# Attention and feed-forward block on one core: the value matmuls of one unit issued in two parts

## The chip, the cores and the metric

The kernel runs on one core of a Trainium2 chip. The metric is the time of one execution on the device in microseconds (us). Profiled times come from one execution under the hardware profiler. TensorE (PE) multiplies matrices; its weight loads (PEld) are listed apart. VectorE (DVE), ScalarE (ACT) and GpSimd (POOL) work elementwise, and SyncE (SP) issues DMAs.

## The reference

Input `x` is 8 x 1024 x 512 in float32. One block is computed:

```
x = x + layernorm(attention(layernorm(x)))
x = x + layernorm(ffn(layernorm(x)))

attention(h):  q, v, k = split(h @ Wqvk)           # 16 heads of 32
               scores  = q . k, causal mask, / sqrt(512)
               weights = softmax(scores over the keys)
               return (weights @ v) @ Wo
ffn(x):        hidden = x @ W1 + b1                # 512 -> 2048
               imag   = w_imag * sin(theta + 0.1 * hidden)
               q      = hidden + 0.1 * (cos(theta) * w_real + sin(theta) * w_imag) * imag
               return relu(q) @ W2 + b2
```

## The kernel before

The batch has eight blocks `b` of 1024 rows. For each, `attention` runs over four groups `g` of four heads, and `feed_forward` follows. Projections of the next group, the rest of the previous block's normalisation and parts of this block's output projection are put between the attention's steps by generators (`work`, `more`), which are advanced at fixed points of the loop. The matmuls, and most of the other instructions near the change, are marked `in_order`: they run on their engine in the order in which the code issues them.

A head group goes in two phases. First `find_maxima` computes the scores with queries on the partitions, to find the row maxima. They are split into bf16 parts (`parts_q`), transposed on TensorE and copied to an SBUF tile `mT`, one for each half of the 1024 queries. For the second half the transposes come in the third unit of the loop below, and the copy is made by VectorE (L734).

Then the loop in `attention` takes the keys in units, with the keys on the partitions. The first half of the queries (`c = 0`) sees key tiles 0 to 3 in three units; the second half (`c = 1`) sees all eight in seven. A counter `at` numbers the ten units from 0 to 9:

```
KEY_UNITS = (
    ((0,), (1, 3), (2,)),
    ((0,), (1,), (2,), (3,), (4,), (5, 7), (6,)),
)
```

Key tile `kb` of 128 keys counts only for queries from `kb` on. So in the first half key tile 1 is 384 queries wide, tile 2 is 256 wide and tile 3 is 128 wide. Unit 1 (`at == 1`) holds tiles 1 and 3 side by side in the 512 columns of a bank.

For each unit the loop does the following, in this order:

- `weigh`: TensorE writes minus the maxima (L603, bf16) and adds the scores (L614, f32). Both use the array as four row tiles (32*128 in the profile), one for each head. They fill two PSUM tiles of two banks each, two heads in each. ScalarE then takes the exponential of each tile (L629) into an SBUF tile `w`. GpSimd sets the squares above the diagonal to zero (L633).
- at some units, the transposes or projections.
- `flush`: runs the step that the previous unit left in `late`. It is `weighted_values`: TensorE multiplies the values with the previous unit's weights (L652), with the array as four column tiles (128*32), and adds them up in one PSUM bank `acc`.
- for the second half, `add_weights`: VectorE adds the unit's weights to the running total (L681).

So TensorE's order is: scores of unit n + 1, values of unit n, scores of unit n + 2, values of unit n + 1. An f32 matmul is two passes and shows as two records. Behind the last unit of the first half ScalarE copies `acc` to `wvT` (L767). The second half's result is divided by its sums in `sums`, which runs in the next group.

`psum` chooses banks by the order in which earlier tiles were drained. Of the eight banks, four hold the scores of a unit, and the next unit's second score tile gets the banks that the first exponential of the unit before sets free.

Of the kernel before, what the change touches and what calls it, by code (L numbers as in the profile page):

```python
# [31 lines left out]
def kernel(  # L32
# [48 lines left out]
    def psum(shape, dtype=F32):  # L81
        size = math.prod(shape[1:]) * (2 if dtype == BF16 else 4)
        n = -(-size // (4 * HALF))
        free = [k for k in range(0, 8, n) if None not in done_at[k : k + n]]

        def rank(k):
            halved = n == 1 and done_at[k ^ 1] is None and done_at[k] + 2 <= clock[0]
            return not halved, max(done_at[k : k + n])

        k = min(free, key=rank)  # L90
        t = banks[:, k : k + n, :].rearrange("p b n -> p (b n)")[:, : size // 4]
        if dtype != F32:
            t = t.bitcast(dtype)
        if len(shape) == 3:
            t = t.rearrange("p (a b) -> p a b", a=shape[1])
        done_at[k : k + n] = [None] * n
        banks_of[id(t)] = list(range(k, k + n)), t
        return t

    def drained(t, n=None):  # L100

        mine = banks_of[id(t)][0]
        for k in [mine[0]] if n is None and len(mine) == 1 else mine if n is None else [mine[n]]:
            clock[0] += 1
            done_at[k] = clock[0]

    def in_order(instruction):
        tc.keep_in_program_order(instruction)
# [180 lines left out]
    def advance(work, steps=1):  # L289
        for _ in range(steps):  # L290
            if next(work, None) is None:
                return

    def finish(work):
        for _ in work:
            pass
# [283 lines left out]
    def transpose_maxima(parts, evacuate):  # L580
        pt = psum([P, TPB, P], BF16)
        for n in range(TPB):
            transpose_on_pe(pt[:, n, :], parts[:, n, :], ident_h)
        mT = small.tile([P, HALF], BF16, tag="mT", name="mT", bufs=2)
        evacuate(mT, pt.rearrange("p n t -> p (n t)"))
        drained(pt)
        return mT
# [58 lines left out]
    def weighted_values(acc, b, g, first, last, weights, placed):  # L646

        for k, (kb, cols, n) in enumerate(placed):
            for j in range(HPG):
                r = slice(j * HD, (j + 1) * HD)  # L650
                in_order(
                    nc.tensor.matmul(  # L652
                        acc[r, HALF - n :],
                        v[b, g][:, kb, r],
                        weights[j // 2][:, j % 2, cols],
                        start=first and k == 0,
                        stop=last and k == len(placed) - 1,
                    )
                )

    def weight_sums(acc, weights, placed):

        for k, (_, cols, n) in enumerate(placed):
            for j in range(HPG):
                r = slice(j * HD, (j + 1) * HD)
                in_order(
                    nc.tensor.matmul(  # L667
                        acc[r, HALF - n :],
                        ones,
                        weights[j // 2][:, j % 2, cols],  # L670
                        start=(k == 0),
                        stop=(k == len(placed) - 1),
                    )
                )

    def add_weights(total, weights, placed):

        for t, w in zip(total, weights):
            for _, cols, n in placed:
                q = slice(HALF - n, HALF)  # L680
                in_order(nc.vector.tensor_add(t[:, :, q], t[:, :, q], w[:, :, cols]))  # L681

    def divide(acc, total, dst):

        inverse = tmp.tile([P, HALF], F32, tag="tmp", name="inverse")
        in_order(nc.scalar.activation(inverse, total, AF.Ln))
        drained(total)
        in_order(nc.scalar.activation(inverse, inverse, AF.Exp, scale=-1.0))
        in_order(nc.vector.tensor_tensor(dst, acc, inverse, ALU.mult))
        drained(acc)  # L690

    def attention(b, wvT, after):

        late = [None]
        summing = [None]

        def sums():
            if summing[0] is not None:  # L700
                summing[0]()
                summing[0] = None

        def flush():
            if late[0] is not None:
                late[0]()
                late[0] = None

        def projections(g):
            if g + 1 < NG:  # L710
                return project_qkv(b, g + 1)
            if g + 1 == NG and b + 1 < B:
                return project_qkv(b + 1, 0)
            return iter(())

        work = projections(0)
        for g in range(NG):
            more, first = after(g)
            mT, later = find_maxima(b, g, work, sums, iter(()) if g and first is not None else more)
            mTs = [mT]  # L720
            at = 0
            for c in range(2):
                accs = []
                total = None
                units = KEY_UNITS[c]
                for u, keys in enumerate(units):
                    later(at)
                    weights, placed = weigh(b, g, c, keys, mTs[c])
                    if at < 2:
                        advance(work)  # L730
                    if at == 2:
                        mTs.append(
                            transpose_maxima(
                                parts_q[1], lambda *a: in_order(nc.vector.tensor_copy(*a))  # L734
                            )
                        )
                    if c and u == len(units) - 2:
                        finish(work)
                        work = projections(g + 1)
                    if c and u >= len(units) - 2:  # L740
                        advance(work)
                    if first is None and (at < 2 or c and u >= len(units) - 2):
                        advance(more)
                    flush()


                    if c and u == 0:
                        total = weights, placed
                    elif c:
                        add_weights(total[0], weights, placed)  # L750

                    def step(accs=accs, u=u, last=u == len(units) - 1, weights=weights, c=c, g=g,
                             placed=placed, total=total, dst=wvT[c][:, g, :]):
                        if u == 0:
                            accs.append(psum([P, HALF]))
                        acc = accs[0]
                        weighted_values(acc, b, g, u == 0, last, weights, placed)
                        if last and c:

                            def whole():  # L760
                                whole_sum = psum([P, HALF])
                                weight_sums(whole_sum, *total)
                                divide(acc, whole_sum, dst)

                            summing[0] = whole
                        elif last:
                            nc.scalar.copy(dst, acc)  # L767
                            drained(acc)

                    late[0] = step  # L770
                    if first is not None and at >= first:
                        advance(more)
                    at += 1
            flush()
            if g == NG - 1:
                advance(more)
                sums()
            else:
                finish(more)
        return more  # L780
# [177 lines left out]
    for b in range(B):  # L958
# [4 lines left out]
        def after(g, b=b, wvT=wvT, x2T=x2T, rest=rest):  # L963


            if g == 0:
                return rest, len(KEY_UNITS[0])
            if (b, g) == (0, 1) and B > 1:
                ahead = measure_ahead(1, (2, 2, 1, 0, 0, 0, 2, 1))
                advance(ahead)  # L970
                return ahead, 2
            if g == NG - 2 and b + 1 < B:
                return norm1(b + 1), None
            if g == NG - 1:
                return finish_block(b, 0, wvT[0], x2T), len(KEY_UNITS[0]) + 1
            return iter(()), 0
# [47 lines left out]
```

## Time and profile before

| | |
|---|---|
| time, median of 3 runs | 3862.25 us (3861.39 to 3862.28) |
| the profiled execution's own time | 3861.85 us |
| its span, first to last instruction | 3860.1 us |
| mean granted TensorE clock | 0.995 |
| PE busy | 3799.7 us (98%) |
| DVE busy | 2743.9 us (71%) |
| ACT busy | 1541.5 us (40%) |
| POOL busy | 576.3 us (15%) |
| DMA | 86.43 MB, mean 22 GB/s |

The profile is that of one execution. In a line of a group, the columns are the line of the code with engine, operation, what is written from what, shape and count; then the busy time in us and the mean of one in ns; then the engine's idle time before these instructions and what released it. In a timeline they are start (us from the start of the span), duration, engine, line and operation; in square brackets the idle time before it and the releaser. Successive pieces of a timeline can overlap a little, since matmuls and elementwise instructions are pipelined and the ends of matmuls are modelled.

### The profile page before, as it was taken

Reading aid. Unit: us, or ns where it says so; the run is one execution under the profiler, and the core shown is the slowest. Engines: PE = TensorE matmul, PEld = TensorE weight load, DVE = VectorE, ACT = ScalarE, POOL = GpSimd, SP = SyncE. Lnnn points to the kernel's source line nnn. Section 1 sums busy time; section 2 is a strip of 40 time slices with the busy share of each in tenths; the row PEclk is TensorE's granted clock in tenths of the full one; section 3 lists DMA queues with packets and bytes.
Section 4 is the critical chain, followed back from the end, with each engine's and each line's share of the span. In section 5 each row is a group of like instructions: output and inputs, shape, how many; then the busy total and the mean of one; then the engine's idle time right before and its main releaser. Section 6 shows DMA issues by size and latency. Waiting matters only on the chain. (4 is left out here: it accounts for less than half of the span.)

```text
span 3860.1 us, 51461 instructions
## 1 busy us (share of the span) xinstructions
PE 3799.7 (98%) x19457; PEld 1767.7 (46%) x19457; DVE 2743.9 (71%) x6105; ACT 1541.5 (40%) x2960; POOL 576.3 (15%) x1060
## 2 busy tenths in 40 slices
PE   8999999999999999999999999999999999999998
PEld 4544445444444444444444444444445444454443
DVE  4867767677676777767777767777677776777666
ACT  4552146521465214642156421564215641156311
POOL 1211021110211102210022100222002120022100
PEclk9999999999999999999999999999999999999999
DMA  4100000000000001000010000000001000000000
GB/s 156 34 12 23 22 31 15 12 22 22 31 15 12 22 22 33 12 12 22 22 34 12 12 22 22 34 12 13 21 22 34 12 12 0 22 23 12 1 0 22
DMA packets 45081, 86.43 MB, mean 22 GB/s; under 512 B 4192, under 2 KB 7328, under 8 KB 44320
## 3 DMA queue, kind: packets, MB, share of 16 engines
q1 hardware_dynamic: 38480, 70.57, 5.6%
q10 hardware_dynamic: 6352, 12.58, 0.9%
q8 instruction: 152, 2.49, 0.3%
q14 instruction: 97, 0.79, 0.1%
HBM read 66.36 MB, written 16.78 MB: 22 GB/s over the span
## 5 line engine op out<-in xcount | busy, mean ns | idle before, releaser
L848 PE MATMUL banks<-x2T,w_sb 128*128 128x512 f32 x2048 | 921.6, 593 | 5.8 <-ACT x2T L266 5.8
L875 PE MATMUL banks<-w_sb,hid 128*128 128x512 f32 x1536 | 690.5, 592 | 0.0
L629 ACT ACTIVATE w<-banks 128x1024 f32<-128x1024 f32 (+1 forms) x640 | 565.2, 935 | 270.8 <-PE banks L614 270.8
L848 PEld LDWEIGHTS banks<-x2T,w_sb 128*128 128x128 f32 x2048 | 386.0, 190 | 478.4 <-issue 468.8
L681 DVE TENSOR_TENSOR w<-w 128x1024 f32<-128x1024 f32 (+2 forms) x448 | 441.3, 1025 | 202.9 <-PE banks L652 157.6
L527 DVE CUSTOM_DVE_ANT_0 es<-banks,mask 128x128 f32<-128x128 f32 (+3 forms) x1024 | 432.9, 485 | 104.3 <-PE banks L497 104.3
L863 ACT ACTIVATE u<-u 128x512 f32<-128x512 f32 x256 | 161.1, 629 | 864.2 <-DVE u L200 840.8
L398 PE MATMUL banks<-xnT,wqvk_sb 128*128 128x512 f32 x1024 | 481.6, 609 | 4.8 <-ACT xnT L266 4.8
L875 PEld LDWEIGHTS banks<-w_sb,hid 128*128 128x128 f32 x1536 | 291.8, 190 | 367.4 <-issue 328.6
L633 POOL TENSOR_SCALAR_AFFINE_SELECT w<-w 128x256 f32<-128x256 f32 x512 | 293.6, 591 | 865.7 <-ACT w L629 814.6
L515 DVE TENSOR_REDUCE mx<-banks 128x1 f32<-128x512 f32 (+1 forms) x384 | 309.6, 862 | 103.9 <-PE banks L497 103.8
L856 ACT ACTIVATE hid<-banks,prm 128x512 f32<-128x512 f32 x256 | 175.7, 686 | 474.5 <-PE banks L848 474.5
L858 DVE TENSOR_SCALAR u<-hid,prm 128x512 f32<-128x512 f32 x256 | 123.8, 484 | 309.8 <-ACT hid L856 309.8
L614 PE MATMUL banks<-qk 32*128 32x512 f32 (+3 forms) x3072 | 332.4, 493 | 0.0
L652 PE MATMUL banks<-w,v 128*32 128x512 f32 (+3 forms) x3072 | 324.9, 502 | 3.8 <-POOL w L633 3.0
L497 PE MATMUL banks<-qk 32*128 32x512 f32 (+3 forms) x3072 | 315.1, 513 | 0.3 <-DVE mx L527 0.2
L866 DVE SCALAR_TENSOR_TENSOR hid<-u,coef,hid 128x512 f32<-128x512 f32 x256 | 191.7, 749 | 162.1 <-ACT u L863 162.0
L398 PEld LDWEIGHTS banks<-xnT,wqvk_sb 128*128 128x128 f32 x1024 | 182.5, 190 | 243.5 <-issue 184.8
L547 ACT ACTIVATE es<-es,mx 128x512 f32<-128x512 f32 (+3 forms) x512 | 279.6, 550 | 2.0 <-DVE mx L527 2.0
L419 PEld LDWEIGHTS banks<-wqvk_sb,xnT 128*128 128x128 f32 x2048 | 239.0, 192 | 50.8 <-issue 23.6
L419 PE MATMUL banks<-wqvk_sb,xnT 128*128 128x128 f32 x2048 | 259.5, 280 | 0.0
L800 PE MATMUL banks<-wo_sb,wvT 128*128 128x512 f32 x512 | 234.3, 600 | 0.0
(102 smaller groups left out, 3401.9 us busy)
## 6 DMA issues: line engine op xcount, KB each, us to landing
xin<-in_L_attn_h_dram SPq DMA_DIRECT2D x112, 256.0 KB, 2.8
out_dram<-x SPq DMA_DIRECT2D x64, 256.0 KB, 2.0
x<-in_L_attn_h_dram SPq DMA_DIRECT2D x60, 256.0 KB, 2.5
w_tail<-in_L_ffn_W_dram SPq DMA_DIRECT2D x8, 1024.0 KB, 5.2
w_sb<-in_L_ffn_W_dram ACTq DMA_DIRECT2D x1, 4096.0 KB, 20.9
w_sb<-in_L_ffn_W_dram ACTq DMA_DIRECT2D x1, 3072.0 KB, 30.4
wqvk_sb<-in_L_attn_Wqvk_dram ACTq DMA_DIRECT2D x3, 768.0 KB, 8.2
x<-in_L_attn_h_dram ACTq DMA_DIRECT2D x4, 256.0 KB, 3.2
```

The source lines that it names most:

```text
L398: nc.tensor.matmul(pq, wqvk_sb[:, kc, c0 : c0 + P], xnT[b, half][:, kc, :], start=(kc == 0), stop=(kc == KC - 1),)
L419: nc.tensor.matmul(pv[:, t - t0, :], xnT[b, t // TPB][:, kc, (t % TPB) * P : (t % TPB + 1) * P], wqvk_sb[:, kc, c0 : c0 + P], start=(kc == 0),
L497: nc.tensor.matmul(scs[j // 2][:, j % 2, at : at + n], t[r, 0, i * P : (i + 1) * P], t[r, 1, k0 : k0 + n], start=True, stop=True,)
L515: nc.vector.tensor_reduce(out=mx[:, m], in_=sc[:, m, cols], op=ALU.min, axis=mybir.AxisListType.X,)
L527: nc.vector.tensor_tensor_reduce(out=es[:, m, cols], in0=sc[:, m, cols], in1=mask[:, HALF - n :], scale=1.0, scalar=FMAX, op0=ALU.add, op1 ...
L614: nc.tensor.matmul(sts[j // 2][:, j % 2, cols], t[r, 1, kb * P : (kb + 1) * P], t[r, 0, q0 : q0 + n], start=False, stop=True,)
L629: in_order(nc.scalar.activation(w[:, :, :width], st[:, :, :width], AF.Exp, scale=-1.0))
L633: select = nc.gpsimd.affine_select(out=square, in_=square, compare_op=ALU.is_ge, fill=0.0, base=0, pattern=[[0, 2], [1, P]], channel_multi ...
L652: nc.tensor.matmul(acc[r, HALF - n :], v[b, g][:, kb, r], weights[j // 2][:, j % 2, cols], start=first and k == 0, stop=last and k == len( ...
L681: in_order(nc.vector.tensor_add(t[:, :, q], t[:, :, q], w[:, :, cols]))
L848: nc.tensor.matmul(ph, w1_sb[:, kc, fc * P : (fc + 1) * P], x2T[half][:, kc, :], start=(kc == 0), stop=(kc == KC - 1),)
L875: nc.tensor.matmul(ys[half, t], hids[c // 2][:, c % 2, t * P : (t + 1) * P], w2_sb[:, fc, :] if fc < NW2 else w2_tail[:, fc - NW2, :], sta ...
```

## The change

At unit 1 the step now issues only the value matmuls of the unit's first key tile (tile 1). Those of the second (tile 3) are put in a list `left`. `flush` issues what is in the list ahead of the step that it runs. The next `flush` after unit 1's step is that of unit 3, which comes after the scores of unit 3, the first ones of the second half. There key tile 3's matmuls precede those of unit 2.

```
         late = [None]
+        left = []
...
         def flush():
+            while left:
+                left.pop()()
             if late[0] is not None:
                 late[0]()
                 late[0] = None
...
-                    def step(accs=accs, u=u, last=u == len(units) - 1, weights=weights, c=c, g=g,
+                    def step(accs=accs, at=at, u=u, last=u == len(units) - 1, weights=weights, c=c, g=g,
                              placed=placed, total=total, dst=wvT[c][:, g, :]):
                         if u == 0:
                             accs.append(psum([P, HALF]))
                         acc = accs[0]
-                        weighted_values(acc, b, g, u == 0, last, weights, placed)
+                        if at == 1:
+
+                            weighted_values(acc, b, g, False, False, weights, placed[:1])
+                            left.append(
+                                lambda: weighted_values(acc, b, g, False, False, weights, placed[1:])
+                            )
+                        else:
+                            weighted_values(acc, b, g, u == 0, last, weights, placed)
```

## The prediction

> **What bounds the kernel now.** I call the ten units of a head group by the code's counter `at`: scores(n) are the matmuls of L603 and L614 of unit n, weights(n) its two ScalarE exponentials (L629), values(n) its matmuls of L652. Values(n) are issued behind scores(n+1). First the page's busy times:
>
> ```profile
> PE 3799.7 (98%) x19457; PEld 1767.7 (46%) x19457; DVE 2743.9 (71%) x6105; ACT 1541.5 (40%) x2960; POOL 576.3 (15%) x1060
> ```
>
> TensorE sets the time, so I looked for where it waits. The groups by shape, engine PE, give the row that matters here (busy and mean, then idle before it and the releaser):
>
> ```profile
> L603 PE MATMUL banks<-mT,minus 32*128 32x512 bf16 x768 | 99.6, 382 | 7.3 <-ACT w L629 7.3
> L652 PE MATMUL banks<-w,v 128*32 128x384 f32 x512 | 64.2, 525 | 1.3 <-POOL w L633 0.5
> L652 PE MATMUL banks<-w,v 128*32 128x128 f32 x512 | 31.7, 285 | 0.7 <-POOL w L633 0.7
> ```
>
> The 7.3 us are 32 gaps of 0.229 us, one in each of the 32 head groups. The timeline of TensorE alone, in one group (block 1, group 1), shows the place:
>
> ```profile
> 612.36 0.60 PE L614 MATMUL banks<-qk 32*128 32x256 f32 x8
> 612.90 0.40 PE L111 MATMUL banks<-ident_h,parts_q 128*128 128x128 bf16 x4
> 613.23 1.07 PE L652 MATMUL banks<-w,v 128*32 128x384 f32 x16
> 614.23 0.40 PE L603 MATMUL banks<-mT,minus 32*128 32x512 bf16 x4
> 614.46 1.03 PE L614 MATMUL banks<-qk 32*128 32x512 f32 x8
> 615.41 0.64 PE L652 MATMUL banks<-w,v 128*32 128x256 f32 x8
> 615.99 0.39 PE L603 MATMUL banks<-mT,minus 32*128 32x512 bf16 x2
> 616.60 0.39 PE L603 MATMUL banks<-mT,minus 32*128 32x512 bf16 x2 [0.23 <-ACT w L629]
> 616.61 1.24 PE L614 MATMUL banks<-qk 32*128 32x512 f32 x8
> 617.78 1.06 PE L652 MATMUL banks<-w,v 128*32 128x512 f32 x8
> ```
>
> The line at 613.23 is values(1): key tile 1 (384 wide) and key tile 3 (128 wide) in one piece. Then come scores(3) at 614.23, values(2) at 615.41, and scores(4) at 615.99, whose second pair of L603 stands until 616.60. The same stretch on ScalarE, VectorE and GpSimd:
>
> ```profile
> 615.53 1.94 ACT L629 ACTIVATE w<-banks 128x1024 f32<-128x1024 f32 x2 [1.43 <-PE banks L614]
> 617.35 0.59 ACT L767 COPY wvT<-banks 128x512 f32<-128x512 f32 x1
> 617.84 1.95 ACT L629 ACTIVATE w<-banks 128x1024 f32<-128x1024 f32 x2
> ```
>
> ```profile
> 613.40 0.42 DVE L734 COPY mT<-banks 128x512 bf16<-128x512 bf16 x1 [0.99 <-PE banks L111]
> 618.95 4.66 DVE L681 TENSOR_TENSOR w<-w 128x1024 f32<-128x1024 f32 x4 [5.12 <-PE banks L652]
> ```
>
> ```profile
> 613.67 0.90 POOL L633 TENSOR_SCALAR_AFFINE_SELECT w<-w 128x256 f32<-128x256 f32 x2 [1.53 <-ACT w L629]
> ```
>
> Scores(4)'s second pair needs the PSUM banks that the first exponential of weights(3) reads. It starts at 615.53, 0.12 us behind scores(3), takes 1.02 us, and TensorE goes on 0.05 us after it. ScalarE had idled 1.43 us before, waiting for scores(3). So the chain here is scores(3), exponential, scores(4), and values(1) stand in front of its first link. Counted from the start of values(1), all 32 groups show scores(3) at 1.00 us (the last group 1.16), the held pair at 3.38 and values(3) at 4.55, each to within 0.01 us.
>
> **The change part by part.**
>
> *What moves.* Key tile 3's value matmuls (four column groups, two passes each for f32, so 8 records) leave values(1) and go behind scores(3), before values(2). The instruction order of the built kernel shows this in all 32 groups and nothing else: same counts, and the other engines' orders and waits unchanged. That it does not do what it says is thus ruled out. No DMA is moved, so SP's queue passes nothing; GpSimd's queue is as it was.
>
> *When scores(3) start.* By the starts of the matmul records in the trace, before: 0.347 us between key tile 1's two passes, 0.323 to key tile 3, 0.109 between its passes, 0.225 to scores(3), together 1.004. After: 0.347, then one gap that the trace lacks, a 384-wide value pass followed by scores. Its nearest rows are the same gap behind other widths: 0.545 (512), 0.332 (256) and 0.225 (128), so 0.107 per 128 columns and 0.12 on top; 384 lies at 0.438. From both sides it is at least the 0.323 of an unchanged kind of matmul and at most 0.545; I take 0.438. Scores(3) start at 0.785, that is 0.22 us earlier per group (bounds 0.11 and 0.33).
>
> *New cover.* The 0.23 us of key tile 3 also covered the VectorE copy of the maxima that scores(3) read (L734): it ends at 613.83, 0.60 after values(1) began, and the tightest starts of TensorE behind VectorE come 0.055 us after its end. Ready at 0.655, needed at 0.785: 0.13 us of cover left, cost nothing. If it were gone, all of TensorE's queue would stand with it. The banks for scores(3)'s second pair come free with weights(2)'s first exponential at 613.61 (0.38): nothing.
>
> *What the moved matmuls cost behind scores(3).* The first pass behind another shape costs 0.025 us more than one running on (256 wide: 0.240 against 0.215), so key tile 3 takes about 0.13 + 0.11 and values(2) 0.215 + 0.33: 0.79 us instead of 0.57. Scores(3) take 1.18 as now, so scores(4)'s first pair starts at 0.785 + 1.18 + 0.79 = 2.76, as before. The held pair follows the exponential and starts at 3.38 - 0.22 = 3.16. So 0.40 us are still free before it: the moved work lies in TensorE's former gap and costs nothing, and would cost something only if it took over 0.40 us more. The gap goes from 0.229 to about 0.01. The waits for GpSimd's selects are met: those of unit 1 end at 612.14 here, those of unit 2 (the row at 613.67) at 614.57, 0.84 us before values(2) start today.
>
> *Behind that.* ScalarE's queue is back to back from weights(3) to weights(4): two exponentials and the copy of the first half's result (L767). That copy waits for values(2), which still end at 2.75, while ScalarE reaches it at 3.9: no wait. VectorE's first addition waits for values(3), with 5.12 us of idle before it, so it moves along. From unit 4 on every stage hangs on TensorE or on this chain, and all moves by 0.22 us.
>
> *The sum.* 32 groups x 0.22 = 7.0 us; the bounds give 3.5 and 10.6. The profiled execution took 3861.85 us (span 3860.1); minus 7.0 that is 3854.85. The median of the runs is 0.4 above the profiled one, so 3855.2.
>
> A rule speaks against it. The Trainium skill, "TensorE: Matmul & The Clock Gate", section "The mechanism", says that a weight load overlaps running matmuls only where it goes to other rows of the array. Value matmuls fill all 128 rows, so by that page none of their loads would be hidden. By the page the time would be that of the slower rival below; by the rows it is the sum above. The trace has this against it: between the last passes of tiles 1 and 3 lie only 0.11 us with four matmuls, though one load takes 0.109; but it shows no 128-wide value pass right behind scores.
>
> **The rivals.**
>
> *Loads exposed (slower).* If a short value pass right behind scores shows its loads one after another, key tile 3 and values(2) need 16 x 0.109 = 1.74 us plus the 0.12 of the change of shape, about 1.84 instead of 0.79. Both pairs of scores(4) then start at 1.97 + 1.84 = 3.81 and not at 3.38: 0.43 us later, x 32 = 14 us, 3876. It decides from 0.62 us of extra time on (the 0.40 free and the 0.22 won). For it: the timeline of weight loads lets value loads start only when scores have ended. Against it: values(2), 256 wide and in the same place today, pay only 0.03 us on their first pass.
>
> *Absorbed.* In steady units VectorE's additions leave no idle time (the stretch of one unit: sum, then PE, PEld, DVE, ACT and POOL busy):
>
> ```profile
> 620.10:622.44 2.34, 2.34 (x22) 0.67 (x20) 2.34 (x4) 1.94 (x2) 0.00 (x0) 1.00 0.00 0
> ```
>
> If they, not TensorE, set when the next group's maxima are taken, the 0.22 us vanish there: 3862.2, or about half, 3858.5, where it holds in some groups. Against it: VectorE waits 104 us for TensorE at the maxima (L527 behind L497), some 3 us per group, and its additions begin earlier too.
>
> *More than forecast.* If the 0.12 us on top of the streaming is not paid behind this shorter piece, scores(3) start at 0.347 + 0.32 = 0.667, just when the maxima are there (0.655): 0.337 us per group, 10.8 us, 3851. For it: the row for 384 is missing. Against it: the three widths that are there lie on one line.
>
> **How the numbers follow.** A measurement of this kernel can tell about 0.2% from no change, 7.7 us. The forecast's 7.0 lies 0.7 inside, 0.02 us per group, which is about the grain of an interpolated gap and of the later stages. So the chain as forecast has 0.76, of which I give 0.27 to a sum over 7.7 and 0.49 to one under it; more than forecast 0.13; absorbed 0.05; loads exposed 0.06. Faster is 0.27 + 0.13 = 0.40, same 0.49 + 0.05 = 0.54, slower 0.06. For the range: from the deeper case at 3851 to the half-absorbed one at 3858.5; what is left out is the slow rival, full absorption and the far end of the fast one, under 0.2. The likeliest case alone is 3854 to 3856.
>
> **What would show it.** In the profile after: L603 512 wide with an idle of under 1 us instead of 7.3; scores(3) at 0.78 and values(3) at 4.33 after the start of key tile 1's matmuls; four 128-wide and four 256-wide matmuls in two passes behind scores(3) in 0.79 us; ScalarE's wait for scores(3) at 1.21 instead of 1.43; the period from group to group 0.22 shorter. It is wrong if scores(3) wait for the VectorE copy, if the moved matmuls last over 1.2 us, or if the groups' periods stay while the gap goes.

## The result and the profile after

The changed kernel takes 3855.19 us (median of 19 runs, 3853.86 to 3856.88) against 3862.25 us before (19 runs). The ratio is 0.9982 with an interval of 0.9976 to 0.9988: 7.1 us or 0.18% less. The prediction was 3855.2. The profiled execution of after took 3853.86 us with a span of 3852.1. It is the fastest of the 19, and its span lies 8.0 us under that of before.

The page's busy times, and the two groups by shape (engine PE) that the prediction named, now read:

```profile
PE 3799.3 (99%) x19457; PEld 1765.1 (46%) x19457; DVE 2743.5 (71%) x6105; ACT 1541.0 (40%) x2960; POOL 574.5 (15%) x1060
```

```profile
L603 PE MATMUL banks<-mT,minus 32*128 32x512 bf16 x768 | 99.6, 382 | 0.3
L652 PE MATMUL banks<-w,v 128*32 128x384 f32 x512 | 64.4, 522 | 1.3 <-POOL w L633 0.5
L652 PE MATMUL banks<-w,v 128*32 128x128 f32 x512 | 32.3, 291 | 0.7 <-POOL w L633 0.7
```

TensorE's busy time is the same to 0.4 us, with the same matmuls; the idle time before L603 has fallen from 7.3 to 0.3 us. The timeline of TensorE, again in block 1, group 1:

```profile
610.95 0.40 PE L111 MATMUL banks<-ident_h,parts_q 128*128 128x128 bf16 x4
611.27 0.85 PE L652 MATMUL banks<-w,v 128*32 128x384 f32 x8
612.06 0.39 PE L603 MATMUL banks<-mT,minus 32*128 32x512 bf16 x4
612.29 1.03 PE L614 MATMUL banks<-qk 32*128 32x512 f32 x8
613.24 0.86 PE L652 MATMUL banks<-w,v 128*32 128x128 f32 x16
614.03 0.79 PE L603 MATMUL banks<-mT,minus 32*128 32x512 bf16 x4
614.44 1.24 PE L614 MATMUL banks<-qk 32*128 32x512 f32 x8
615.61 1.06 PE L652 MATMUL banks<-w,v 128*32 128x512 f32 x8
```

Key tile 1 alone starts at 611.27, scores(3) 0.79 us later instead of 1.00. The moved matmuls and values(2) are the one line at 613.24. Scores(4) start at 614.03; their second pair is still held, by 0.40 us (it starts at 614.43), but the profile gives the first pair a duration of 0.39 us, so that almost nothing of the hold is seen as idle. So the four L603 are now one line. Values(3) start 4.34 us behind key tile 1 instead of 4.55. ScalarE and VectorE in the same stretch:

```profile
613.36 1.94 ACT L629 ACTIVATE w<-banks 128x1024 f32<-128x1024 f32 x2 [1.22 <-PE banks L614]
615.18 0.59 ACT L777 COPY wvT<-banks 128x512 f32<-128x512 f32 x1
615.67 1.95 ACT L629 ACTIVATE w<-banks 128x1024 f32<-128x1024 f32 x2
```

```profile
616.78 5.83 DVE L681 TENSOR_TENSOR w<-w 128x1024 f32<-128x1024 f32 x5 [4.90 <-PE banks L652]
```

ScalarE waits 1.22 us for scores(3) instead of 1.43. The first addition comes 5.51 us behind key tile 1 instead of 5.72. From group to group the period is 0.21 to 0.25 us shorter everywhere but at the end: the period that ends in the last group loses 0.47, and the stretch from there to the end 0.02. In the last group key tile 1's second pair itself waits for GpSimd's selects, and scores(3) start at 1.18. From the first to the last group the gains of the periods sum to 7.1 us. Another 0.8 us between the two profiled spans lies ahead of the first group, where nothing was changed.

### The profile page after: what moved, and what is told of

It reads as the page before. It is cut to its first block, busy times and chain, and to the rows that moved or that the text cites. A ratio compares the mean times of both kernels' runs of the same rounds, so it can differ in the third digit from the quotient of the medians.

```text
span 3852.1 us, 51461 instructions
## 1 busy us (share of the span) xinstructions
PE 3799.3 (99%) x19457; PEld 1765.1 (46%) x19457; DVE 2743.5 (71%) x6105; ACT 1541.0 (40%) x2960; POOL 574.5 (15%) x1060
## 5 line engine op out<-in xcount | busy, mean ns | idle before, releaser
L614 PE MATMUL banks<-qk 32*128 32x512 f32 (+3 forms) x3072 | 332.2, 492 | 0.0
```

The source lines that it names most:

```text
L614: nc.tensor.matmul(sts[j // 2][:, j % 2, cols], t[r, 1, kb * P : (kb + 1) * P], t[r, 0, q0 : q0 + n], start=False, stop=True,)
```

## The experiments

The theory is the prediction's chain: scores(3), exponential, scores(4) set the time of this stretch, and what stands in front of scores(3) is paid while what stands between scores(3) and scores(4) is free up to a limit. Its main rival is that TensorE is full, so that only its visible idle time can be won and every matmul counts. The steady period, below, is the median time from one head group to the next. All times below of the form "at 3.06" count, as in the prediction, from the point at which value matmuls can start behind the transposes. Each kernel was compared with before on its own chip.

| run | time, us | before, us | ratio (interval) |
|---|---|---|---|
| e1_tile1_late | 3854.54 | 3862.4 | 0.998 (0.9971 to 0.9988) |
| e2_all_late | 3861.72 | 3862.4 | 0.9998 (0.9989 to 1.0007) |
| e3_tile3_twice | 3855.42 | 3862.4 | 0.9982 (0.9973 to 0.9991) |
| e4_tile3_four_times | 3865.94 | 3862.4 | 1.001 (1.0001 to 1.0019) |
| e5_change_again | 3855.17 | 3862.93 | 0.9982 (0.9973 to 0.9991) |
| e6_split_columns | 3850.29 | 3862.93 | 0.9969 (0.9957 to 0.998) |
| e7_copy_on_vector | 3855.77 | 3862.93 | 0.9982 (0.9973 to 0.9991) |
| e8_split_and_copy | 3851.52 | 3862.93 | 0.9971 (0.996 to 0.9983) |

### Key tile 1 late instead of key tile 3

```
-    weighted_values(acc, b, g, False, False, weights, placed[:1])
+    weighted_values(acc, b, g, False, False, weights, placed[1:])
     left.append(
-        lambda: weighted_values(acc, b, g, False, False, weights, placed[1:])
+        lambda: weighted_values(acc, b, g, False, False, weights, placed[:1])
     )
```

> The parts are swapped: key tile 3's value matmuls stay in front of scores(3), key tile 1's go behind. Chain theory (the time hangs on scores(3), exponential, scores(4)): TensorE needs only 0.13 + 0.23 = 0.36 us after the transposes, so scores(3) now wait for the VectorE copy and start at 0.655 instead of 1.00. The values behind them take 0.347 + 0.323 + 0.215 + 0.332 = 1.22 us, so scores(4) start at 1.84 + 1.22 = 3.06, just when the exponential is done (3.03), all four L603 together; values(3) start at 4.24 instead of 4.55: 0.31 us per group, -10 us against before (3852.3). Rival, visible idle (only the 7.3 us that TensorE is seen to stand can be won, and new standing in front of scores(3) is paid): 0.30 us of new idle per group against 0.23 taken away, 3864.

It took 7.9 us less than before, not 10. The group by shape and the timelines of TensorE and ScalarE (block 1, group 1, whose key tile 3 starts at 613.38):

```profile
L603 PE MATMUL banks<-mT,minus 32*128 32x512 bf16 x768 | 89.9, 382 | 7.1 <-DVE mT L737 7.1
```

```profile
614.03 0.40 PE L603 MATMUL banks<-mT,minus 32*128 32x512 bf16 x4 [0.23 <-DVE mT L737]
...
616.43 0.39 PE L603 MATMUL banks<-mT,minus 32*128 32x512 bf16 x4
616.66 1.02 PE L614 MATMUL banks<-qk 32*128 32x512 f32 x8
617.61 1.07 PE L652 MATMUL banks<-w,v 128*32 128x512 f32 x8
618.61 0.64 PE L603 MATMUL banks<-mT,minus 32*128 32x512 bf16 x4
```

```profile
617.14 0.59 ACT L777 COPY wvT<-banks 128x512 f32<-128x512 f32 x1
617.79 1.94 ACT L629 ACTIVATE w<-banks 128x1024 f32<-128x1024 f32 x2
```

The visible idle time is back at 7.1 us, now on the VectorE copy, and yet the kernel is as fast as the change: the rival's 3864 is out. Up to values(3), at 617.61 or 4.23, every time is the forecast one to 0.01 us. Then a part is lost: scores(5)'s pairs start 0.25 us apart instead of 0.14. The reason is in weights(4). Its first exponential reads the first pair's two heads only, and starts at 617.79, 4.41: no earlier than in the change (4.40). In the change the first pair's L603 is done ahead, while the second is held, so its L614 start with the held pair's release (3.16) and its second pass at 3.70. Here all four L603 start at 3.06, L614 0.23 us later, and the first pair's second pass at 3.71. So the link is the first pair, and not the end of scores(4); my figure of 0.31 us was taken at the wrong point. The steady period falls by 0.21 us, as weights(4) do (4.41 against 4.62). Some of the 7.9 us comes from elsewhere: the seven periods that lead from one block to the next fall by 0.30 to 0.33 and the last one by 1.0. Why they do is open.

### All of unit 1 late

```
-    weighted_values(acc, b, g, False, False, weights, placed[:1])
     left.append(
-        lambda: weighted_values(acc, b, g, False, False, weights, placed[1:])
+        lambda: weighted_values(acc, b, g, False, False, weights, placed)
     )
```

> All of unit 1's value matmuls go behind scores(3). Chain theory: scores(3) wait for the VectorE copy and start at 0.655; the values behind them take 0.347 + 0.323 + 0.109 + 0.109 + 0.215 + 0.332 = 1.43 us, longer than the exponential, so scores(4) start at 1.84 + 1.43 = 3.27 with both pairs and values(3) at 4.45 instead of 4.55: 0.10 us per group, -3 us against before (3859), that is 4 us slower than the change. Rival, visible idle: 0.6 us of new standing in front of scores(3) against 0.23 taken away, +12 us (3874). A second rival, cover does not matter (scores(3) start right behind the transposes): -10 us or more.

```profile
L603 PE MATMUL banks<-mT,minus 32*128 32x512 bf16 x768 | 89.7, 382 | 18.6 <-DVE mT L737 18.6
```

In one group, whose value matmuls could start at 612.85:

```profile
613.50 0.40 PE L603 MATMUL banks<-mT,minus 32*128 32x512 bf16 x4 [0.58 <-DVE mT L737]
...
616.12 0.39 PE L603 MATMUL banks<-mT,minus 32*128 32x512 bf16 x4
...
617.30 1.06 PE L652 MATMUL banks<-w,v 128*32 128x512 f32 x8
```

```profile
617.48 1.94 ACT L629 ACTIVATE w<-banks 128x1024 f32<-128x1024 f32 x2 [0.27 <-PE banks L614]
```

The idle row shows 18.6 us, 0.58 per group, where before had 7.3, and the time is that of before within the interval: visible idle is no price. Scores(3) start at 0.65, so the copy is their limit, and the second rival (cover doesn't matter) is out too. Values(3) start at 4.46, as forecast, but weights(4) at 4.63 against 4.62 before, again by the first pair (L603 at 3.27, second pass at 3.93). So the whole 0.35 us that scores(3) won is given back where the values outlast the exponential. The time alone does not part the forecast 3859 from no change, both of which lie in the interval. The steady period does: it grows by 0.01 us, as weights(4) do, where the forecast had it fall by 0.10.

### The moved matmuls two and four times

```
-        lambda: weighted_values(acc, b, g, False, False, weights, placed[1:])
+        lambda: weighted_values(acc, b, g, False, False, weights, placed[1:] * 2)
```

> As the change, but key tile 3's value matmuls behind scores(3) are issued twice, so that key tile 3 counts twice in the first half. Chain theory: 0.22 us more of TensorE work per group (7 us in all) fits into the 0.40 us that are free ahead of the held pair of scores(4): first pair at 2.98, held pair still at 3.16, values(3) at 4.33; same time as the change, 3855.2. Rival, TensorE is full (98% busy) and every matmul counts: +7 us, 3862.

The other run has `* 4`. Both add key tile 3 to the first half's result more than once, so their output is not that of the block.

> As the change, but key tile 3's value matmuls behind scores(3) are issued four times, so that key tile 3 counts four times in the first half. Chain theory: 0.65 us more per group, 0.40 of it free: scores(4) start at 3.41 with both pairs instead of 3.16 for the held one, values(3) at 4.59: +0.26 us per group, +8 us against the change, 3863.5. Rival, every matmul counts: +21 us, 3876.

Twice cost nothing (3855.42): scores(4)'s first pair starts at 2.98, the held one at 3.16 and values(3) at 4.33, as forecast. The page's first line for it:

```profile
PE 3799.2 (99%) x19713; PEld 1772.2 (46%) x19713; DVE 2743.3 (71%) x6105; ACT 1541.5 (40%) x2960; POOL 575.5 (15%) x1060
```

There are 256 records more than in the change, 0.22 us per group by their starts, and the busy time is the same: what the profile of the change calls busy held 7 us in which matmuls were held. The Trainium skill, "Trainium Kernel Development and Optimization", section "Performance Expectations", calls matmul busy time a bad metric for how close a kernel is to roofline, with pipelining as its reason. The trace agrees that it is bad, with 3799.2 and 3799.3 us for two kernels that lie 7 us of matmuls apart; here the reason is the hold.

Four times took 10.6 us more than the change, each against before on its own chip; the forecast had 8 and the rival 21. TensorE and ScalarE in one group, whose key tile 1 starts at 613.96:

```profile
615.92 1.51 PE L652 MATMUL banks<-w,v 128*32 128x128 f32 x40
617.37 0.39 PE L603 MATMUL banks<-mT,minus 32*128 32x512 bf16 x4
617.60 1.03 PE L614 MATMUL banks<-qk 32*128 32x512 f32 x8
```

```profile
617.86 0.59 ACT L777 COPY wvT<-banks 128x512 f32<-128x512 f32 x1
618.73 1.94 ACT L629 ACTIVATE w<-banks 128x1024 f32<-128x1024 f32 x2 [0.27 <-PE banks L614]
```

Scores(4) start at 3.41, as forecast. Weights(4) start at 4.77 instead of 4.40, 0.37 us later, x 32 = 12 us. With 0.65 us added and 0.37 paid, 0.28 us were free and not 0.40: the first pair has to start some 0.12 us ahead of the held pair's release. In the change and in the run with twice, with leads of 0.40 and 0.18 us, the first pair's second pass starts 0.54 us behind that release; without a hold, in E1, E2 and here (E4), it starts 0.655 us behind the first pair's own L603.

The periods settle whether the first pair or the end of scores(4) is the link:

| against before, us | values(3) | weights(4) | steady period |
|---|---|---|---|
| the change | -0.22 | -0.22 | -0.22 |
| e1_tile1_late | -0.32 | -0.20 | -0.21 |
| e2_all_late | -0.10 | +0.01 | +0.01 |
| e4_tile3_four_times | +0.04 | +0.15 | +0.15 |

The period follows weights(4), which hang on the first pair, and not values(3), which follow the end of scores(4).

### The split that this points to, and the copy in ScalarE's queue

If the first pair is the link, the best order has scores(3) at the copy's limit and few enough values behind. So only key tile 1's last 256 columns stay in front:

```
-    weighted_values(acc, b, g, False, False, weights, placed[:1])
+    kb, cols, n = placed[0]
+    tail = slice(cols.start + P, cols.stop)
+    weighted_values(acc, b, g, False, False, weights, [(kb, tail, n - P)])
...
+    left.append(rest)     # key tile 1's first 128 columns, then placed[1:]
```

The copy's run changes one line, and the fourth kernel has both edits:

```
-    nc.scalar.copy(dst, acc)
+    in_order(nc.vector.tensor_copy(dst, acc))
```

> The change itself, on the chip of the next three: 3855 us, 7 us under before, both theories.

> As the change, but of key tile 1 only its last 256 query columns stay in front of scores(3); its first 128 go behind with key tile 3. First-pair theory (what sets weights(4) is the second pass of scores(4)'s first pair, which needs its own L603 done 0.23 us earlier and the held pair's release): scores(3) start at 0.655, the values behind them take 0.133 + 0.109 + 0.109 + 0.109 + 0.215 + 0.332 = 1.01 us, scores(4)'s first L603 start at 2.85, the held pair at 3.02, the first pair's L614 at 3.08, its second pass at 3.58 and the exponential at 4.28 instead of 4.40: 0.12 us per group, 4 us under the change, 3851. Rival, end of all scores(4) sets what follows: values(3) at 3.02 + 1.17 = 4.19 instead of 4.33, 0.14 us per group and about the same time, but then the swapped order of before should have won 10 us and not 8. Second rival, the copy of the first half's result in ScalarE's queue sets weights(4): no more than 4 us, with the exponential right behind the copy.

> As the change, but the copy of the first half's result (0.59 us on ScalarE, between weights(3) and weights(4)) is made by VectorE, which idles there. First-pair theory: weights(4) wait for TensorE (second pass at 3.70, exponential 0.70 behind it at 4.40), the copy only fills a wait; same time as the change, 3855. Rival, ScalarE's queue binds: weights(4) start earlier and the time falls by 2 us or more, 3853.

> Split columns and the copy on VectorE together. First-pair theory: as split columns, 3851, with the exponential at 4.28. Rival, ScalarE's queue binds in the split: another 2 us or more, 3849.

The change took 3855.17 again. The split took 3850.29, 12.6 us under before, 4.9 under the change, and the fastest kernel of the study. Its TensorE and ScalarE:

```profile
612.40 0.64 PE L652 MATMUL banks<-w,v 128*32 128x256 f32 x8
613.06 0.40 PE L603 MATMUL banks<-mT,minus 32*128 32x512 bf16 x4
613.27 1.04 PE L614 MATMUL banks<-qk 32*128 32x512 f32 x8
614.24 0.43 PE L770 MATMUL banks<-w,v 128*32 128x128 f32 x8
614.48 0.83 PE L652 MATMUL banks<-w,v 128*32 128x128 f32 x16
615.25 0.56 PE L603 MATMUL banks<-mT,minus 32*128 32x512 bf16 x4
```

```profile
616.17 0.59 ACT L792 COPY wvT<-banks 128x512 f32<-128x512 f32 x1
616.66 1.95 ACT L629 ACTIVATE w<-banks 128x1024 f32<-128x1024 f32 x2
```

By the medians of the 32 groups scores(3) start at 0.65 and scores(4) at 2.85, as forecast. Weights(4) start at 4.25, 0.03 us ahead of the forecast 4.28, since the forecast asked for a lead of 0.23 us, and the 0.17 that the first pair has here is enough. The period falls by 0.36 us per group against before, 0.14 more than in the change. Values(3) move by 0.14 as well (4.33 to 4.19), so this run does not part the first pair from the end of scores(4) as the link; the table above does.

The split also takes key tile 1's diagonal square, which GpSimd sets, out of what stands in front of scores(3): in the last group scores(3) start at 0.58, right behind the copy, instead of 1.18. The period that ends there falls by 1.25 us against before and the stretch behind it by 0.6, which the forecast had not counted. How much of this is the split's is not shown: in the profile of the change's second run (e5) scores(3) of the last group start at 0.78, the period that ends there is 0.33 longer than in before and the stretch behind it 0.39 shorter.

With the copy on VectorE (3855.77) nothing is won, and ScalarE shows why (key tile 1 starts at 611.20):

```profile
613.28 1.94 ACT L629 ACTIVATE w<-banks 128x1024 f32<-128x1024 f32 x2 [1.22 <-PE banks L614]
615.60 1.94 ACT L629 ACTIVATE w<-banks 128x1024 f32<-128x1024 f32 x2 [0.38 <-PE banks L614]
```

Where the copy stood there is now a wait for TensorE, and weights(4) start at the same 4.40. So ScalarE's queue, back to back as it was, set nothing: copy and matmul chain ended together. Both edits (3851.52) put weights(4) at 4.25: again the split's gain alone, with no further one. The rival that the copy binds is out in both.

## Why the prediction was right

- **The interpolated gap.** The 384-wide value pass followed by scores, put at 0.438 us on a line through three other widths, is 0.438 in the trace (median of 32). This gave 0.22 us per group.
- **The cover of the copy.** 0.13 us were left, and scores(3) did not wait. E1 and E2 show the limit: there scores(3) wait for the copy, which ends at 0.60, and start at 0.65.
- **The moved matmuls.** Scores(4)'s first pair starts at 2.76, the held one at 3.16 and values(3) at 4.33 to 4.34, each as written. Key tile 3's two passes behind scores are 0.133 us apart and the next piece follows 0.109 later. So the rival of exposed loads does not occur. In E4 eight such passes follow each other at about 0.11 us, with four loads of 0.11 us in each, which start while the pass before them runs. The rule of the Trainium skill ("TensorE: Matmul & The Clock Gate", "The mechanism"), that loads overlap only with matmuls on other rows, does not hold for these column tiles.
- **Behind that.** All later stages moved along; the periods say so. The absorbed case did not occur: VectorE's additions just begin earlier.
- **The sum.** 7.0 us predicted, 7.06 measured by the medians. In the profile the last two stretches lost 0.47 and 0.02 instead of 0.22 each, which by luck comes to nearly the same sum. The ends differ between executions: in the profile of e5, the same kernel, the first of them grew by 0.33 and the second lost 0.39.

Three things in the working were less exact than the number. The 0.11 us that the prediction puts between the last passes of tiles 1 and 3 lie between the two passes of tile 3; the argument stands with it. The 0.40 us said to be free for the moved work were 0.28 (E4), because the first pair needs its lead of 0.12. And the prediction let the held pair stand for the whole of scores(4). In the change the two agree, since the first pair's L603 still start 0.40 us ahead of the held pair; in E1, E2 and E4 they don't, and there the same reasoning gave 10, 3 and 8 us where 7.9, 0.7 and 10.6 were measured.

## What to carry to other kernels

In a loop in which two engines feed each other, work on one of them is paid or free by where it stands: in front of the piece that the other engine waits for it is paid, behind it and in the other's shadow it is free. Lay the starts of both engines' pieces in one row, find which half of a piece the next engine really needs, and move work across until the shadow is just full; a visible idle row says where to look, not what can be won. The rows of one shape at several widths give the price of a width that the trace lacks.

## What the runs showed of the hardware

- A change from column tiles to row tiles costs about 0.12 us over the streaming (0.107 us per 128 columns) at every width seen: 0.225, 0.332, 0.438 and 0.545 us behind passes of 128, 256, 384 and 512 columns.
- A held matmul can hide in the busy time. The change still holds scores(4)'s second pair by 0.40 us with an idle row of 0.3 us in all, and 256 records more left the busy time at 3799 us.
- The first exponential starts 0.64 us behind the first pair's second pass for scores(3), but 0.70 for scores(4), with the copy in ScalarE's queue or without it, and with a held pair or without one. Why was not tried.
